# A transformer block with expert routing on one Trainium2 core: the jobs of an expert cut into sixteen equal slots

## The chip, the cores and the metric

The kernel runs on one core of one Trainium2 chip. The metric is the device time of one execution in microseconds (us). The engines are TensorE (PE in the profile, with its weight loads as PEld), VectorE (DVE), ScalarE (ACT), GpSimd (POOL) and SyncE (SP), which here only issues DMAs.

## The reference

The input is 16 sequences of 256 tokens with 256 features (4096 tokens). Attention with 16 heads comes first, then a mixture of 8 experts in which the expert chooses its tokens:

```python
x = x + o @ Wout.T                                    # attention
tok = x.reshape(-1, d)                                # 4096 tokens
gate = softmax(tok @ Wgate.T, axis=-1)                # 4096 x 8
k_cap = bs // E                                       # 512 tokens for an expert
vals, idx = top_k(gate.T, k_cap)
w, idx_flat = vals.T, idx.T.reshape(-1)
g = _ln(tok[idx_flat], mlp_g, mlp_b).reshape(k_cap, E, d)
y = gelu(einsum('ked,ehd->keh', g, fc1s) + b1s)       # 256 -> 1024
y = (einsum('keh,edh->ked', y, fc2s) + b2s) * w[..., None]
tok = tok.at[idx_flat].add(y.reshape(-1, d))
```

All arithmetic that matters for the output is float32. Lists and one-hots of the routing are bfloat16.

## The kernel before, in words

**Two parts of the choice.** The tokens form 32 tiles of 128. The kernel does not wait for the last sequence before it starts the experts: a first routing chooses, for each expert, the best 256 among the first 30 tiles, and a second routing chooses the other 256 among all 32 tiles less those already chosen. That gives 16 jobs of 256 tokens each: jobs 0 to 7 are the eight experts with the first routing (30 tiles), jobs 8 to 15 the eight experts with the second (32 tiles).

**Order of the work.** Each engine works through its instructions in the order in which the Python code emits them. Up to job 0 this order comes from a plan with due times, written out by hand (`at(...)`, sorted in L1064); the change leaves it alone. From L1090 on the order is that of the last loop, `for k in range(1, len(jobs))`. It starts at about 970 us of a span of 1232.7 us.

**A routing.** `Gates` turns the logits of some tiles into gate values: `shift` (VectorE), `exp` (ScalarE), `divide` (VectorE) and `parts` (GpSimd, which splits each gate value into three bfloat16 parts). `Routing.turn` transposes the gate values on TensorE, and `evict` copies them out. Then a binary search over 30 bits finds the threshold of each expert. A bit has four steps: `compare` (VectorE, L776: which values reach the candidate, and how many in each partition), `count` (TensorE, L783: a small bfloat16 product that adds up the partitions), `drop` (VectorE, L788) and `step` (VectorE, L795), which give the next candidate. At the end come `masks` (VectorE), `totals` (TensorE), `place` (VectorE, two scans), `turn_places` (TensorE) and `split` (VectorE), which give each chosen token its place in the list. The second routing runs inside the last loop; `second_routing` is a generator that hands out its steps.

**A job** (class `Job`) consists of these steps:

- `load`: SyncE issues the DMAs of both weights (1 MB each) and of the second bias. Each of the two weight buffers is one of two, so the load of job k+2 waits for the products of job k.
- `gives` (VectorE, L879 and L887): the values that the list product carries, token numbers and gate parts.
- `onehot(a, b)` (VectorE, L897): for the tiles a to b-1 a 128x128 bfloat16 one-hot of each token's place.
- `list_matmul(a, b)` (TensorE, L906): one small bfloat16 product for each tile, a 128x128 one-hot against 10 columns, all added up in one PSUM tile. The result is the list of the job's tokens.
- `take` (VectorE, L914 to L920) copies the list, forms the indices and the weights `w`; `gather` (GpSimd, L925) fetches the 256 normalised tokens by two indirect DMAs.
- `transposes` (TensorE, L934, four) and `evict` (VectorE, L941, two) bring the gathered tokens into the form `xT`.
- `up(f)` (TensorE, L953) for f = 0 to 7: four float32 half products of 256 columns into a PSUM tile; `gelu(f)` (ScalarE, L960).
- `down(i, a, b)` (TensorE, L969) for i = 0 and 1: two half products for each hidden chunk f.
- `finish(i)` (VectorE, L975 and L976): bias and gate weight; `scatter(i)` (GpSimd, L979): an indirect DMA that adds the rows to the output.

**The last loop.** A pass k runs the products of job k (called `a`) and prepares job k+1 (`new`) and job k+2 (`far`). Over the eight up steps it places the second half of the one-hots of `new` (four after each of the first four steps) and its list products (six after each of the first six steps); `take` and `gather` of `new` come after the seventh up step. In the down part it places `transposes` and `evict` of `new` in the middle of the second output half, and the `gives` and first half of the one-hots of `far`, eight in each half. `route_on()` stands ahead of each up step and twice in each down half, 12 times in a pass, and emits one step of the second routing each time: for a bit, `compare` is one step, and `count`, `drop` and `step` together are the next. So a pass does six bits, and the second routing ends in pass 6. In that pass the preparation of job 8, the first with the second routing, stands behind the end of the routing.

Of the kernel before, what the change touches and what calls it, by code (L numbers as in the profile page):

```python
# [25 lines left out]
NT = NTOK // P  # L26
# [3 lines left out]
FC = DD // P  # L30
KC = CAP // P
KL = KC // 2
# [11 lines left out]
def kernel(  # L44
# [329 lines left out]
    if True:  # L374
# [370 lines left out]
        class Routing:  # L745
# [46 lines left out]
            def step(self, n):  # L792

                old, self.cand = self.cand, bit.tile([P, 1], I32, tag="cand", name="cand")
                nc.vector.scalar_tensor_tensor(  # L795
                    self.cand, self.dropped, (1 << n) >> 1, old,
                    ALU.bitwise_or, ALU.bitwise_xor,
                )
# [207 lines left out]
        for b in range(B):  # L1006
# [3 lines left out]
            a = First(b)  # L1010
# [4 lines left out]
            for (g, t), p in its["group"].items():  # L1015
                a = Group(b, g, t)
# [6 lines left out]
            for (d, *ij), p in its["quad"].items():  # L1023
                a = quads[d]
# [6 lines left out]
            for t in range(TB):  # L1031
                a = Tail(b, t)
# [7 lines left out]
        stretches = [Gates(0, n0), Gates(n0, n1), Gates(n1, NT)]  # L1040
# [3 lines left out]
        second = Routing(first)  # L1044
# [5 lines left out]
        jobs = [Job(e, r, n) for r, n in ((first, n1), (second, NT)) for e in range(E)]  # L1050
# [15 lines left out]

        def second_routing():
            a = stretches[2]  # L1070
            yield from (a.shift, a.exp, a.divide, a.parts, second.turn, second.evict)
            for n in range(29, -1, -1):
                yield partial(second.compare, n)

                def decide(n=n):
                    second.count(n)
                    second.drop(n)
                    second.step(n)
                yield decide
            yield from (second.masks, second.totals, second.place, second.turn_places,  # L1080
                        second.split)

        rest = second_routing()

        def route_on(n=1):
            for step in (next(rest, None) for _ in range(n)):
                if step:
                    step()

        jobs[2].load()  # L1090
        jobs[2].gives()
        jobs[2].onehot(0, NT // 2)
        for k in range(1, len(jobs)):
            a = jobs[k]
            new = jobs[k + 1] if k + 1 < len(jobs) else None
            far = jobs[k + 2] if k + 2 < len(jobs) else None
            for f in range(FC):
                route_on()
                a.up(f)
                a.gelu(f)  # L1100
                if new:
                    if f < 4:
                        new.onehot(NT // 2 + 4 * f, NT // 2 + 4 * f + 4)
                    if f < 6:
                        new.list_matmul(6 * f, 6 * f + 6)
                    if f == 6:
                        new.take()
                        new.gather()
            for i in range(KL):
                route_on()  # L1110
                a.down(i, 0, FC // 2)
                if new and i == KL - 1:
                    new.transposes()
                    new.evict()
                route_on()
                if far and k != len(jobs) // 2 - 2:
                    if i == 0:
                        far.gives()
                    far.onehot(i * NT // 4, (i + 1) * NT // 4)
                a.down(i, FC // 2, FC)  # L1120
                a.finish(i)
                a.scatter(i)
            if k == len(jobs) // 2 - 2:
                while (step := next(rest, None)):
                    step()
                far.gives()
                far.onehot(0, NT // 2)
            if far:
                far.load()


# [47 lines left out]
```

## Time and profile before

| what | us |
|---|---|
| median of 3 runs | 1235.27 (1234.18 to 1235.83) |
| profiled execution | 1234.45 |
| its span in the profile | 1232.70 |
| TensorE busy, of the span | 1180.2 (96%) |
| VectorE busy | 773.4 (63%) |
| ScalarE busy | 603.0 (49%) |
| GpSimd busy | 592.6 (48%) |
| first up product of job 1 | 969.98 |
| first up product of job 15 | 1208.97 |
| from the first up product of job 1 to that of job 8 | 123.72 |
| from the first up product of job 8 to that of job 15 | 115.26 |

Durations that the profile gives for one instruction of the expert part: an up half product is busy 393 ns and a weight load 190 ns; both are pipelined, so the step from one start to the next is shorter. A list product is busy 168 ns, a one-hot 259 ns, `compare` 476 ns, `drop` 154 ns, `step` 165 ns.

How to read it: a timeline line has the start in us from the span's start, the length, the engine, the line of the kernel, the operation, the tile written and the tiles read, and a number of instructions (x4). In brackets stands the time for which the engine sat idle just before and what ended that wait. A row by windows has the stretch, its length, and then for each engine the time busy and the number of instructions; after these the granted clock of TensorE (1.00 is full), the busy share of the DMA engines and the rate in GB/s. A line of waits has the waiting instruction, the one it waited for, the total, how often and the longest.

### The profile page before, as it was taken

What the parts mean: (1) busy time and instruction counts of PE and PEld (TensorE: products, weight loads), DVE (VectorE), ACT (ScalarE), POOL (GpSimd) and SP (SyncE); (2) the same over time, 40 slices, a digit from 0 to 9 for tenths busy, and PEclk for the clock granted to TensorE, in tenths of its full rate; (3) what the DMA queues carried; (4) which work ended last, traced back from release to release, by engine and by line L of the source; (5) the groups of instructions that cost most, each with busy time, mean ns of one, the idle gap of its engine ahead of it and who ended that gap; (6) DMA issues with size and microseconds to landing.
All of it is one profiled execution on the core that took longest, in us unless ns stands there. A gap on an engine that the chain in (4) does not pass through costs nothing. (4 is left out here: it accounts for less than half of the span.)

```text
span 1232.7 us, 19466 instructions
## 1 busy us (share of the span) xinstructions
PE 1180.2 (96%) x6784; PEld 814.0 (66%) x6784; DVE 773.4 (63%) x2276; ACT 603.0 (49%) x1669; POOL 592.6 (48%) x818
## 2 busy tenths in 40 slices
PE   6999999999999999999999999999978999999996
PEld 3556666766566666667575766667646777788875
DVE  7556665757566666657665666665776567755551
ACT  2665555555555555555555555657551322122221
POOL 4555555645555555555455555556653232323322
PEclk9999999999999999999999999999997999999999
DMA  5000000000000000000000000000201556556551
GB/s 181 1 1 5 22 10 18 9 18 14 14 27 1 26 5 23 9 18 14 13 15 14 26 6 22 6 14 18 90 1 46 186 140 177 153 161 178 154 164 26
DMA packets 46739, 62.41 MB, mean 51 GB/s; under 512 B 3888, under 2 KB 39984, under 8 KB 46640
## 3 DMA queue, kind: packets, MB, share of 16 engines
q1 hardware_dynamic: 39808, 52.70, 12.8%
q0 software_dynamic: 6144, 8.39, 3.9%
q8 instruction: 54, 0.88, 0.3%
q14 instruction: 45, 0.37, 0.1%
q10 hardware_dynamic: 688, 0.06, 0.0%
HBM read 48.56 MB, written 12.58 MB: 50 GB/s over the span
## 5 line engine op out<-in xcount | busy, mean ns | idle before, releaser
L608 POOL TENSOR_SCALAR pr<-pr,sums 128x256 f32<-128x256 f32 x512 | 240.0, 489 | 275.1 <-DVE sums L604 259.1
L506 PE MATMUL pm<-wq,hT 128*128 128x512 f32 x768 | 356.8, 603 | 5.0 <-DMA wq<-in_wqkvT 3.0
L597 ACT ACTIVATE pr<-sc,nmax 128x256 f32<-128x256 f32 x512 | 236.9, 477 | 161.4 <-DVE nmax L588 147.0
L82 POOL TENSOR_TENSOR ss<-ss,neghalf 128x8 f32<-128x8 f32 x128 | 210.6, 1650 | 97.8 <-DVE ss L527 95.0
L506 PEld LDWEIGHTS pm<-wq,hT 128*128 128x128 f32 x768 | 137.8, 192 | 148.2 <-issue 135.5
L588 DVE TENSOR_REDUCE nmax<-sc 128x2 f32<-128x512 f32 x256 | 164.5, 681 | 44.7 <-PE sc L581 44.5
L960 ACT ACTIVATE hid<-ph,vec 128x256 f32<-128x256 f32 x128 | 60.3, 474 | 212.7 <-PE ph L953 205.3
L523 DVE TENSOR_REDUCE ss<-sq 128x8 f32<-128x512 f32 x128 | 87.4, 682 | 108.8 <-ACT sq L519 108.6
L617 PEld LDWEIGHTS pp<-ident,pr 128*128 128x128 f32 x1024 | 120.0, 144 | 35.0 <-issue 20.1
L617 PE MATMUL pp<-ident,pr 128*128 128x128 f32 x1024 | 140.0, 277 | 3.3 <-ACT pr L597 2.5
L635 PE MATMUL po<-prT,v 128*64 128x256 f32 x1024 | 139.4, 395 | 0.7 <-ACT oT L645 0.7
L953 PE MATMUL ph<-xT,w 128*128 128x256 f32 x512 | 131.7, 393 | 0.1
L581 PE MATMUL sc<-kT,qT 64*128 64x256 f32 x1024 | 130.2, 392 | 0.0
L519 ACT ACTIVATE sq<-pm 128x512 f32<-128x512 f32 x128 | 77.2, 603 | 90.4 <-PE pm L506 89.2
L659 PE MATMUL pw<-wo,oT 128*128 128x256 f32 x512 | 118.5, 384 | 0.0
L581 PEld LDWEIGHTS sc<-kT,qT 64*128 64x128 f32 x1024 | 94.2, 187 | 34.7 <-issue 23.6
L969 PE MATMUL py<-w,hid 128*128 128x256 f32 x512 | 116.9, 381 | 0.0
L979 POOL DMA_INDIRECT out<-y,idx x32 | 51.1, 1598 | 121.4 <-DVE y L976 62.7
L597 ACT ACTIVATION_READ_ACCUMULATOR pr<-sc,nmax 128x1 f32 x512 | 105.9, 207 | 0.0
L659 PEld LDWEIGHTS pw<-wo,oT 128*128 128x128 f32 x512 | 95.7, 192 | 13.0 <-issue 0.8
L625 DVE COPY prT<-pp 128x512 f32<-128x512 f32 x112 | 76.9, 687 | 43.4 <-PE pp L617 42.5
L969 PEld LDWEIGHTS py<-w,hid 128*128 128x128 f32 x512 | 95.6, 190 | 12.7
(118 smaller groups left out, 1312.1 us busy)
## 6 DMA issues: line engine op xcount, KB each, us to landing
w<-in_fc1T SPq DMA_DIRECT2D x16, 1024.0 KB, 5.5
w<-in_fc2T SPq DMA_DIRECT2D x16, 1024.0 KB, 5.6
xs<-in_x SPq DMA_DIRECT2D x16, 256.0 KB, 2.9
out<-tok SPq DMA_DIRECT2D x32, 128.0 KB, 1.7
xn_dram<-tn SPq DMA_DIRECT2D x32, 128.0 KB, 1.7
wq<-in_wqkvT SPq DMA_DIRECT2D x6, 512.0 KB, 8.6
b<-in_b2s SPq DMA_DIRECT2D x16, 128.0 KB, 5.2
wo<-in_woutT SPq DMA_DIRECT2D x1, 1024.0 KB
```

The source lines that it names most:

```text
L82: nc.gpsimd.tensor_tensor(dst, src, neghalf[:, : src.shape[1]], ALU.pow)
L506: nc.tensor.matmul(self.pm, hTs[self.b][:, c, bass.ts(self.t, P)], wq[:, c, bass.ts(self.g, GW)], start=(c == 0), stop=(c == DC - 1),)
L523: nc.vector.tensor_reduce(self.ss[:, 0, :], self.sq.rearrange("p (h d) -> p h d", d=HD), AX.X, ALU.add,)
L581: nc.tensor.matmul(self.sc[i, j][:, t, :], qTs[self.b][rows, hp, bass.ts(t, P)], kTs[self.b][rows, hp, :], start=True, stop=True,)
L588: nc.vector.tensor_reduce(self.nmax[i, j], self.sc[i, j], AX.X, ALU.max, negate=True)
L597: nc.scalar.activation(self.pr[i, j][:, t, :], self.sc[i, j][:, t, :], AF.Exp, bias=self.nmax[i, j][:, t : t + 1], scale=1.0, accum_out=se ...
L608: nc.gpsimd.tensor_scalar(self.pr[i, j][:, t, :], self.pr[i, j][:, t, :], self.sums[i][:, 1, j, t : t + 1], 1.0, ALU.mult, ALU.mult,)
L617: nc.tensor.transpose(self.pp[i, j][:, c, bass.ts(t, P)], self.pr[i, j][:, t, bass.ts(c, P)], ident,)
L635: nc.tensor.matmul(self.po[j * HD : (j + 1) * HD, i, :], vs[self.b][:, c, bass.ts(4 * self.d + 2 * i + j, HD)], self.prT[i, j][:, c, :], s ...
L659: nc.tensor.matmul(self.pw, oTs[self.b][:, hp, bass.ts(self.t, P)], wo[:, hp, :], start=(hp == 0), stop=(hp == HP - 1),)
L953: nc.tensor.matmul(self.ph[f], self.w1[:, c, bass.ts(f, P)], self.xT[:, c, :], start=(c == 0), stop=(c == DC - 1),)
L969: nc.tensor.matmul(self.py[i], self.hid[:, f, bass.ts(i, P)], self.w2[:, f, :], start=(f == 0), stop=(f == FC - 1),)
```

## The change

A pass now has 16 slots: one for each of the eight up steps, and eight for the down part, each with two of the eight hidden chunks of one output half (`down(i, 2 * q, 2 * q + 2)`). `second_routing` yields a list of steps for each slot, and these are emitted at the head of the slot, ahead of its products. A bit takes two slots: in the first stand `count`, `drop` and `step` of one bit and the `compare` of the next, the second is empty. So a pass does eight bits; the whole takes 74 slots, and ends in slot 9 of pass 5. In pass 1 the gate steps stand in slots 0 to 2 and `turn` in slot 4.

The list products of `new` stand in one cluster of 30 or 32 at the head of slot 6, with `take` and `gather` right behind. The one-hots of `new` come four in each of slots 0 to 3, as before. In pass 7, where job 8 is `new` (`late`), `gives` and all 32 one-hots stand in slots 0 to 3, eight in each, and the cluster in slot 7. `transposes` and `evict` of `new` stand at the head of slot 14, in the middle of the second output half as before. For `far`, `gives` stands in slot 9 and the one-hots, four at a time, in slots 10, 12, 13 and 15; pass 6 has none. `finish(0)` and `scatter(0)` stand at the end of slot 11, `finish(1)` and `scatter(1)` at the end of slot 15.

```diff
@@ -1066,27 +1066,21 @@
         def second_routing():
-            a = stretches[2]
-            yield from (a.shift, a.exp, a.divide, a.parts, second.turn, second.evict)
+            a, b = stretches[2], second
+            yield from ([a.shift], [a.exp], [a.divide, a.parts], [], [b.turn], [b.evict])
+            new = [partial(b.compare, 29)]
             for n in range(29, -1, -1):
-                yield partial(second.compare, n)
-
-                def decide(n=n):
-                    second.count(n)
-                    second.drop(n)
-                    second.step(n)
-                yield decide
-            yield from (second.masks, second.totals, second.place, second.turn_places,
-                        second.split)
+                yield new
+                yield []
+                new = [partial(f, n) for f in (b.count, b.drop, b.step)]
+                new.append(partial(b.compare, n - 1) if n else b.masks)
+            yield from (new, [], [b.totals, b.place], [], [], [], [b.turn_places], [b.split])
         rest = second_routing()
-
-        def route_on(n=1):
-            for step in (next(rest, None) for _ in range(n)):
-                if step:
-                    step()
-
+        last = len(jobs) // 2 - 2
         jobs[2].load()
         jobs[2].gives()
         jobs[2].onehot(0, NT // 2)
@@ -1094,39 +1088,41 @@
             a = jobs[k]
             new = jobs[k + 1] if k + 1 < len(jobs) else None
             far = jobs[k + 2] if k + 2 < len(jobs) else None
-            for f in range(FC):
-                route_on()
-                a.up(f)
-                a.gelu(f)
-                if new:
-                    if f < 4:
-                        new.onehot(NT // 2 + 4 * f, NT // 2 + 4 * f + 4)
-                    if f < 6:
-                        new.list_matmul(6 * f, 6 * f + 6)
-                    if f == 6:
-                        new.take()
-                        new.gather()
-            for i in range(KL):
-                route_on()
-                a.down(i, 0, FC // 2)
-                if new and i == KL - 1:
+            late = k == last + 1
+            for s in range(2 * FC):
+                for step in next(rest, ()):
+                    step()
+                if new and s < 4:
+                    if late and s == 0:
+                        new.gives()
+                    h = 0 if late else NT // 2
+                    w = (NT - h) // 4
+                    new.onehot(h + w * s, h + w * s + w)
+                if new and s == (7 if late else 6):
+                    new.list_matmul(0, NT)
+                    new.take()
+                    new.gather()
+                if new and s == 14:
                     new.transposes()
                     new.evict()
-                route_on()
-                if far and k != len(jobs) // 2 - 2:
-                    if i == 0:
+                if far and k != last and s in (9, 10, 12, 13, 15):
+                    if s == 9:
                         far.gives()
-                    far.onehot(i * NT // 4, (i + 1) * NT // 4)
-                a.down(i, FC // 2, FC)
-                a.finish(i)
-                a.scatter(i)
-            if k == len(jobs) // 2 - 2:
-                while (step := next(rest, None)):
-                    step()
-                far.gives()
-                far.onehot(0, NT // 2)
+                    else:
+                        w = {10: 0, 12: 1, 13: 2, 15: 3}[s]
+                        far.onehot(w * NT // 8, (w + 1) * NT // 8)
+                if s < FC:
+                    a.up(s)
+                    a.gelu(s)
+                else:
+                    i, q = divmod(s - FC, 4)
+                    a.down(i, 2 * q, 2 * q + 2)
+                    if q == 3:
+                        a.finish(i)
+                        a.scatter(i)
             if far:
                 far.load()
+        assert next(rest, None) is None
 def kernel(**inputs):
```

## The prediction, made before the change was run

> **What bounds the kernel now.** The change lies in the last fifth of the span, where expert jobs 1 to 15 run one after the other. I write job k for pass k of the last loop, and call its period the time from its first up product to the first up product of job k+1. I read the busy time by windows first, one window per period: span, then TensorE, weight loads, VectorE, ScalarE, GpSimd.
>
> ```profile
> 1023.13:1040.56 17.43, 16.22 (x106) 13.51 (x105) 12.43 (x67) 3.80 (x8) 5.21 (x4) 1.00 0.59 160
> ...
> 1110.36:1126.69 16.33, 15.80 (x102) 13.27 (x101) 8.83 (x45) 3.80 (x8) 5.18 (x4) 1.00 0.59 170
> ...
> 1193.39:1208.97 15.58, 15.58 (x102) 13.32 (x101) 6.24 (x30) 3.80 (x8) 5.18 (x4) 1.00 0.41 105
> ```
>
> These are jobs 4, 9 and 14. TensorE sets the end everywhere; the periods differ by what it waits for. All 14 periods in us: 18.56, 17.36, 17.23, 17.42, 17.14, 17.42, 18.59 (jobs 1 to 7, sum 123.72), 16.65, 16.32, 16.52, 16.39, 17.41, 16.39, 15.58 (jobs 8 to 14). Next TensorE's waits from 970 to 1209 us:
>
> ```profile
> PE px L934 <- DMA xg<-xn_dram,idx: 6.0, 9, 1.6
> PE pc L783 <- DVE reach L776: 4.7, 5, 0.9
> PE pls L906 <- DVE oh L897: 2.5, 4, 1.0
> ```
>
> So: the gather, the search's count, and the one-hots (jobs 1 and 7). Last, the timelines. TensorE in job 9, start and length first:
>
> ```profile
> 1108.25 0.55 PE L934 MATMUL px<-ident,xg 128*128 128x128 f32 x3 [0.86 <-DMA xg<-xn_dram,idx]
> ...
> 1110.36 1.03 PE L953 MATMUL ph<-xT,w 128*128 128x256 f32 x4
> 1111.22 0.30 PE L906 MATMUL pls<-give,oh 128*128 128x10 bf16 x6
> 1111.38 1.11 PE L953 MATMUL ph<-xT,w 128*128 128x256 f32 x4
> ```
>
> An up step is four f32 half products, 0.2155 us apart (0.862). List products follow one another at 0.025. After a cluster the second f32 half comes 0.299 after the first, not 0.2155. So a cluster of n costs 0.087 + 0.025n: six cost 0.24, and 0.862 + 0.24 is the 1.10 from the up step at 1111.38 to the next at 1112.48. The same view of job 4, then VectorE there:
>
> ```profile
> 1025.23 0.16 PE L783 MATMUL pc<-cnt,block 128*128 128x1 bf16 x1 [0.93 <-DVE reach L776]
> ```
>
> ```profile
> 1023.97 0.41 DVE L975 TENSOR_TENSOR y<-py,b 128x256 f32<-128x256 f32 x1
> 1024.42 0.35 DVE L976 TENSOR_SCALAR y<-y,w 128x256 f32<-128x256 f32 x1
> 1024.69 0.47 DVE L776 TENSOR_SCALAR_CACHE_REDUCE reach<-gT,cand 128x256 bf16<-128x256 f32 x1
> ...
> 1025.74 0.15 DVE L788 TENSOR_SCALAR drop<-pc 128x1 int32<-128x1 f32 x1
> ```
>
> The count waits because its compare stands on VectorE behind the last job's `finish`. From start to start: y to scale 0.45, scale to the next 0.27 (finish 0.72); drop to step 0.18, step to compare 0.19, compare to the next 0.40 (a bit 0.77); compare to the count on TensorE 0.54; a one-hot 0.163. The end of a list copies to `ls` 0.21 later, and from `ls` to the second gathered half at TensorE are 7.4 to 8.1 us, 8.7 once. In job 14, with no weights in flight, the gather holds nothing up.
>
> **The Trainium skill.** "TensorE: Matmul & The Clock Gate", section "Wait — 56ns, not 53.3ns?", gives a floor of about 25 ns from product to product, which the trace shows, and about 62 ns a product where the sequencer decodes in software. The trace's longest run at 0.025 is ten; a run of 32 is not shown. Its opening table gives TensorE a queue of 64, and the others one of 8 in strict order; that VectorE works in order is what the lines above show. The same page, "What's actually happening", has the clock halved after an idle window of 3.41 us. The trace has such windows, but half idle is enough (busy TensorE, then its clock):
>
> ```profile
> 896.55:899.96 3.41, 1.39 (x10) 1.00 0.00 0
> 899.96:903.38 3.42, 3.21 (x14) 0.50 0.00 0
> ...
> 1173.03:1176.44 3.41, 1.80 (x11) 1.00 0.38 48
> ```
>
> Busy 1.39 was followed by half clock, and so were 1.66 and 1.49 later (920.44, 940.92); 1.78 (from 893.14) and 1.80 were not.
>
> **The change, part by part.** *Jobs 8 to 14, one cluster.* Six clusters become one: 5 x 0.087 = 0.435 saved. The one-hots are in place: finish ends 0.9 into the job (on VectorE only four far one-hots stand ahead of it now), the 16 left take 2.6, so 3.6, and the cluster comes after six up steps, at 5.17. Is the gain eaten by the gather? List end, gather, and the weight load behind the eighth up step all move by the same 0.435, and TensorE's work from list end to transposes is unchanged, so the wait of 0.1 to 1.9 there stays as it is. VectorE's new order (eight one-hots between finish and evict) is done 7.5 after list end, the transposes at 8.5. On GpSimd the gather stays behind the same scatter; SP's loads keep their place. 7 x 0.435 = **3.05 saved**.
>
> *Job 6.* The search ends in slot 9 of job 5 (74 slots, 16 a job), so job 6 has neither search nor far one-hots: list end 5.17 + 0.78 = 5.95, second gathered half 5.95 + 0.21 + 7.7 = 13.86, next job 0.28 + 1.83 later: 15.97. **1.45 saved**.
>
> *Job 7.* gives and all 32 one-hots lie in its slots 0 to 3: finish 0.92, gives 0.80, one-hots 5.12 (jitter of the same 32 in job 7 of before), 0.30 to TensorE: list end 7.14, 0.3 later than slot 7 alone gives. + 0.21 + 7.6 + 0.28 + 1.83 = 17.06; the gather now starts with the weight load and not ahead of it, 0 to 0.6 more; I take 0.14: 17.2. **1.39 saved**.
>
> *Jobs 2 to 4, eight bits each, not six.* A wait in order again, now: drop blocks VectorE's queue, and behind it stand compare, the one-hots and evict. I walk VectorE from the count of slot 12 (time 0). finish(0) is ready at 0.20, drop 0.92, compare done 1.69, eight one-hots 2.99, drop and compare of slot 14 3.77, evict (TensorE had its transposes at 2.85, gather included) to 4.68, next job's up at 4.81, four one-hots 5.33, finish 6.05, compare at TensorE: count of slot 2 at 6.96. Then eight one-hots and a bit, 2.07, against two slots and a count on TensorE, 1.84: count of slot 4 at 9.03, of slot 6 at 11.10, list end 11.85, slot 8 at 13.68, and slot 12, 3.67 later, at 17.35. That is the period, against 17.34 on average now: eight counts and VectorE's chain eat the 0.35 of the clusters. **0.04 lost** over three jobs.
>
> *Job 5.* The masks take 0.8 in place of a compare, so totals start about 0.6 after TensorE is there; `place` (2.84, as in job 6 of before) now stands ahead of `take` on VectorE, which starts 1.2 after list end + 0.21. The gather is late by that: 18.28. **1.14 lost**.
>
> *Job 1.* Up to gate_of VectorE's queue is the same, so turn cannot start before it does now:
>
> ```profile
> 976.47 0.51 PE L757 MATMUL pgT<-ident,gate_of 128*128 128x128 f32 x2 [0.19 <-DVE gate_of L727]
> ```
>
> What filled TensorE till then, 24 list products and the waits for them, is gone: it is through up steps 0 to 3 at about 973.6 and idles 2.9. The lists come after turn: list end 979.25, not 977.81; with VectorE's chain as above, 8.48 from the count of slot 8 to the next up: 19.58. **1.02 lost**. And 2.9 idle: unless the free-running window splits it evenly, one window has under 1.7 busy, and half clock follows: 3.41 x 0.5 = 1.7 at most, nothing if split. Bounds 0 and 1.7; about four in five positions trigger it; I take **1.4 lost**, an estimate.
>
> Sum: 3.05 + 1.45 + 1.39 - 0.04 - 1.14 - 1.02 - 1.4 = **2.3 us saved**. The profiled execution took 1234.45 (span 1232.70 and 1.75 around it), so 1232.15 there; the median of the runs is 0.8 above it: 1235.27 - 2.3 = **1233.0 us**.
>
> **The unknown costs.** Products 11 to 32 of a cluster: 25 ns (none in the trace is faster) to 62; I take 25, since a queue of 64 holds 32 pairs and TensorE runs 0.2155 a pair before them. VectorE's walk: half a microsecond a job either way.
>
> **Rivals.** *B, slower: the cluster starves.* If TensorE's queue holds few pairs, products past the tenth come at 62 ns: 37 x 22 x 14 = 11.4, thus 1244. It decides from 7.5 ns more per product (308 of them) on, and is slower by 0.2% from 15.5. For it: no run over ten. Against: runs of ten at 0.025 without a sign of tiring. *C: two slots are enough.* If VectorE's chain does not bind, jobs 2 to 4 fall to the gather's floor (list end 6.17, + 0.21 + 7.55 + 0.28 + 1.83 = 16.04), 3.9 less: 1229.1. Against it stand finish and eight one-hots in the queue. *D: the change doesn't do what it says,* jobs 8 to 13 keep their periods since the gather lands when the weights are through: 6 x 0.435 given back, 1235.6. Job 14, without weights, speaks for it; that the load moves along speaks against. *E:* more half-clock windows or a later gather in jobs 5 and 7: 1236 to 1238.
>
> **Chances.** Forecast 0.62 (own range 1231 to 1235), B 0.12, C 0.13, D 0.06, E 0.07. About 0.2%, 2.5 us, is what a measurement can tell from no change: under 1232.8 is faster. The forecast straddles it: 0.30 faster, 0.31 same, 0.01 slower; C faster; B 0.10 slower, 0.02 same; D same; E 0.05 slower, 0.02 same: 0.43, 0.41, 0.16. Range 1229 to 1237: it leaves out most of B, half of C and some of E, 0.19.
>
> **What would show it.** Right: list runs of 32 at 0.025 and periods 0.435 shorter in jobs 8 to 14; turn still near 976.5 with 2.9 idle before it, half clock behind; jobs 2 to 4 near 17.35 with counts waiting 0.2 to 0.4 for reach; `ls` waiting behind `place` in job 5. Wrong: spacing over 0.03 inside the cluster, search jobs near 16, or clean jobs with a longer gather wait than now.

## The result, and the profile after

The changed kernel takes 1229.72 us (median of 5 runs, 1227.31 to 1231.03) beside 1235.83 of the kernel before (5 runs): ratio 0.9951, 95% interval 0.9936 to 0.9965, so 6.1 us faster, with 4.3 and 7.9 as the ends. The forecast was 1233.0 and 2.3 us faster. The direction and the range held; the size was off by nearly 4 us, and 1233.0 itself lies outside the interval.

The profiled execution took 1229.52 us, its span 1227.8. Busy times are nearly those of before (TensorE 1175.4, VectorE 777.0). The windows of jobs 4, 9 and 14 after the change, columns as before:

```profile
1023.93:1041.13 17.20, 16.36 (x108) 13.27 (x107) 14.23 (x75) 3.79 (x8) 5.20 (x4) 1.00 0.55 162
...
1108.29:1124.21 15.92, 15.35 (x101) 13.30 (x100) 9.02 (x45) 3.79 (x8) 5.17 (x4) 1.00 0.61 174
1188.77:1203.91 15.14, 15.14 (x102) 13.35 (x100) 5.68 (x26) 3.79 (x8) 5.18 (x4) 1.00 0.42 108
```

Job 14 is 0.44 shorter, as forecast, and job 4 hardly changed although it now does eight bits. TensorE's waits in the whole stretch (968 to 1204 us) show what changed places:

```profile
PE px L934 <- DMA xg<-xn_dram,idx: 6.9, 8, 1.7
PE pgT L757 <- DVE gate_of L727: 2.9, 1, 2.9
PE pc L783 <- DVE reach L776: 2.4, 4, 0.6
PE po L813 <- DVE mask L806: 0.5, 1, 0.5
PE ph L953 <- DVE xT L941: 0.5, 3, 0.2
```

The wait of the lists for one-hots is gone, that of the count is halved, and a new one of 2.9 us stands ahead of turn in job 1. TensorE's timeline in job 9:

```profile
1106.18 0.55 PE L934 MATMUL px<-ident,xg 128*128 128x128 f32 x3 [0.78 <-DMA xg<-xn_dram,idx]
...
1108.29 5.34 PE L953 MATMUL ph<-xT,w 128*128 128x256 f32 x24
1113.47 0.95 PE L906 MATMUL pls<-give,oh 128*128 128x10 bf16 x32
1114.27 1.97 PE L953 MATMUL ph<-xT,w 128*128 128x256 f32 x8
```

All 32 list products run in 0.80 us up to the next up product, 0.025 each to the last: no product of the cluster is slower. The wait for the gather stays.

To see what repeats, both kernels were profiled a second time in the experiments. The periods in us, as in the prediction:

| jobs | before | before again | forecast | after | after again |
|---|---|---|---|---|---|
| 1 | 18.56 | 18.55 | 20.98 | 20.91 | 19.22 |
| 2 to 4 | 52.01 | 52.64 | 52.05 | 51.63 | 51.63 |
| 5 | 17.14 | 17.23 | 18.28 | 17.35 | 17.55 |
| 6 | 17.42 | 17.42 | 15.97 | 16.03 | 15.85 |
| 7 | 18.59 | 20.03 | 17.2 | 17.64 | 17.56 |
| 8 to 14 | 115.26 | 115.10 | 112.21 | 111.76 | 111.61 |
| 1 to 14 | 238.98 | 240.97 | 236.69 | 235.32 | 233.42 |

The means of the last row differ by 5.6 us, which is most of the measured 6.1. The rest can't be read from four traces: the stretch ahead of job 1, which the change leaves alone, scatters by 4 us (job 1 begins at 969.98 and 966.17 us in the traces of before, at 968.59 and 970.23 in those of after).

### The profile page after: what moved, and what is told of

Its sections match the earlier page's. It is cut to its first block, busy times and chain, and to the rows that moved or that the text cites. A ratio compares the mean times of both kernels' runs of the same rounds, so it can differ in the third digit from the quotient of the medians.

```text
span 1227.8 us, 19464 instructions
## 1 busy us (share of the span) xinstructions
PE 1175.4 (96%) x6784; PEld 812.7 (66%) x6784; DVE 777.0 (63%) x2276; ACT 602.2 (49%) x1669; POOL 590.7 (48%) x818
## 5 line engine op out<-in xcount | busy, mean ns | idle before, releaser
L953 PE MATMUL ph<-xT,w 128*128 128x256 f32 x512 | 121.0, 388 | 0.6 <-DVE xT L941 0.5
L953 PEld LDWEIGHTS ph<-xT,w 128*128 128x128 f32 x512 | 95.7, 192 | 17.8 <-issue 3.5
```

The source lines that it names most:

```text
L953: nc.tensor.matmul(self.ph[f], self.w1[:, c, bass.ts(f, P)], self.xT[:, c, :], start=(c == 0), stop=(c == DC - 1),)
```

## The experiments

All edits but one are made to the changed kernel. The ratio is to the kernel before, timed on the same chip; its medians were 1234.6, 1234.7, 1235.7 and 1234.6 in the four groups of runs. The groups ran on three chips, so kernels of two groups are best compared by their ratios. The trace of a kernel is one execution.

### Both kernels again

No edit.

> The changed kernel once more, nothing edited, to see what repeats. Theory (the change saves about 3.7 us in jobs 1 to 14, the rest of the measured 6.1 is spread of the runs and of waits on gathers): 3 to 7 us under the kernel before; in the trace job 1 takes 20.5 to 21 with 2.9 us idle ahead of turn, jobs 2 to 5 take 17.2 to 17.4, and the periods of jobs 7 to 13 scatter by some tenths with the gather. First up product of job 1 anywhere between 968 and 970.5, since nothing ahead of it was changed. Rival (the change does something ahead of job 1): it stands near 968.6 again, and that of the kernel before near 970 in every trace.

> The kernel before once more, nothing edited. Theory (what lies ahead of job 1, and the gather's landing, scatter from run to run): within 1.5 us of the other runs of the kernel before; the first up product of job 1 between 968 and 971, job 12 near 16.5 and not 17.4 again, the other periods within 0.5 us of the first trace. Rival (these differences belong to the kernel): job 1 begins near 970.0 and job 12 takes 17.4 again.

The changed kernel: 1227.82 us, ratio 0.9943 (0.9923 to 0.9963). The kernel before: 0.9996 (0.9985 to 1.0008). The first up product of job 1 stood between 966.2 and 970.3 in all traces of this study: the spread ahead of job 1 is not the change's, though it is wider than expected (the second trace of before begins at 966.17, below the 968 given). Two periods missed as well: job 1 of the changed kernel took 19.22, not 20.5 to 21, and job 7 of the kernel before 20.03, not within 0.5 of 18.59; both are a matter of half clock, below. And job 12 was wrong: it took 17.41, 17.54, and 17.25 in the cluster-alone kernel below, that is, in every kernel with the old places of the one-hots, and 15.4 to 16.6 in all others. There the second gathered half of job 13 lands 8.7 to 9.0 us after its `ls` (the copy of the list), elsewhere 7.4 to 8.3. The line from the trace of before:

```profile
1174.89 0.55 PE L934 MATMUL px<-ident,xg 128*128 128x128 f32 x3 [1.61 <-DMA xg<-xn_dram,idx]
```

So about 1.1 us of the gain is this one gather. It goes with the slots and not with the cluster, as the traces of both parts alone show (one each, below); why it does is open.

### The cluster in jobs 8 to 14

```diff
                 if new and s == (7 if late else 6):
-                    new.list_matmul(0, NT)
+                    if not (k > 7):
+                        new.list_matmul(0, NT)
...
                     a.up(s)
                     a.gelu(s)
+                    if new and (k > 7) and s < 6:
+                        new.list_matmul(6 * s, 6 * s + 6)
```

> The changed kernel, but in passes 8 to 14 the list products stand six behind each of the first six up steps, as before the change. Theory (each cluster costs TensorE 0.087 us beside 0.025 per product, and the gather moves along with the list's end): those seven periods are 0.435 longer each, 3.0 us in all. Rival (the gather lands when the weights are through, and takes the clusters' gain back): jobs 8 to 13 keep their periods, only job 14 is 0.44 longer, and the time moves by less than 0.6 us.

1232.61 us, 0.9980 (0.9971 to 0.9989), 4.8 slower than the changed kernel beside it. Jobs 9 to 14 take 98.05 us, 6 x 0.40 more than the 95.62 of the first trace after (6 x 0.46 more than the second), and job 14 alone 0.44 more. A half-clock window behind the wait of job 7 adds 0.8 to job 7 and as much to job 8, and is more than half of the 1.4 by which job 8 is longer; how often it falls in the other runs, and so how much of the 4.8 it makes, is not known. The theory holds; the rival, no change in jobs 8 to 13, falls.

### The wait ahead of turn, two ways

Lists of pass 1 spread (the edit of the last experiment with `k == 1` for `k > 7`), and TensorE kept at work:

> The changed kernel, but in pass 1 alone the 30 list products stand six behind each of the first six up steps, as before the change. Theory (clustering left TensorE nothing to do ahead of turn, which VectorE sets): job 1 falls from 20.9 to about 18.2 us (the idle stretch of 2.9 is gone, no window of half clock behind it, the list ends 1.5 us sooner), so 2.7 us faster. Rival (turn sets the job's length, whatever lies ahead of it): within 0.5 us of the changed kernel.

```diff
+            def fill():
+                idle = ps.tile([P, CAPL], F32, tag="mm", bufs=3, name="idle")
+                for _ in range(6):
+                    nc.tensor.matmul(
+                        idle, jobs[1].w1[:, 0, :P], jobs[1].xT[:, 0, :], start=True, stop=True
+                    )
-            yield from (..., [b.turn], [b.evict])
+            yield from (..., [fill, b.turn], [b.evict])
```

> The changed kernel with six float32 products of 128x256 on TensorE, into a tile that nobody reads, ahead of turn in pass 1: 2.6 us of the 2.9 that TensorE idles there are filled, and turn starts when it did. Theory (a window that is half idle is followed by half clock, which costs up to 1.7 us here): no half clock after it, job 1 about 19.5 in place of 20.9, 1.4 us faster. Rival (half clock costs nothing, the job waits for VectorE and the gather anyway): job 1 stays at 20.9 though the clock is full.

Half clock is a granted clock of 0.50. In the traces it begins at the edge of a regular stretch of 3.41 us, and such a stretch is called a window here.

Spread: 1225.86 us, 0.9930 (0.9911 to 0.9950); job 1 takes 18.78, with no half clock. Filled: 1225.66, 0.9928 (0.9910 to 0.9945); job 1 takes 19.28, with no half clock. Both medians are about 2 us under the changed kernel beside them, though the intervals overlap. TensorE in the spread kernel, then in the filled one:

```profile
973.35 0.51 PE L757 MATMUL pgT<-ident,gate_of 128*128 128x128 f32 x2 [0.19 <-DVE gate_of L727]
```

```profile
970.07 2.75 PE L1076 MATMUL idle<-xT,w 128*128 128x256 f32 x12
973.20 0.48 PE L757 MATMUL pgT<-ident,gate_of 128*128 128x128 f32 x2 [0.38 <-DVE oh L897]
```

Turn comes 6.5 to 6.6 us into the job in both: VectorE sets it. The half clock is best read from the two traces of the changed kernel. Windows of the clock, TensorE's busy time and then the clock, first trace and second:

```profile
975.08 0.55 PE L757 MATMUL pgT<-ident,gate_of 128*128 128x128 f32 x2 [2.88 <-DVE gate_of L727]
```

```profile
972.00:975.42 3.42, 0.54 (x3) 1.00 0.82 236
975.42:978.83 3.41, 3.41 (x10) 0.50 0.32 34
```

```profile
971.87:975.28 3.41, 1.98 (x10) 1.00 1.00 323
975.28:978.70 3.42, 1.98 (x10) 1.00 0.29 52
```

The same wait of 2.88 falls into one window in the first and into two equal parts in the second. The first is followed by half clock, the second is not: job 1 takes 20.91 and 19.22, so half clock costs 1.69 here. Of the seven traces of kernels with this wait and no filler, six have half clock behind it; job 1 took 20.29 to 20.74 in the other five. Beside the 19.22 without half clock the filled kernel wins nothing in job 1 and the spread kernel 0.4, so what both gain there is mainly that half clock stayed away: the filler's theory holds and its rival falls, while the spread's 2.7 was too much. (The filled kernel's job 2 takes 18.28, 1.1 longer, with a late gather.) And spreading doesn't rule half clock out: in the kernel with all lists spread, below, job 1 takes 19.85 with a half-clock window in it.

### Job 8 prepared like the others

```diff
-        last = len(jobs) // 2 - 2
+        last = -2
```

> The changed kernel without the special case of job 8: its gives and the first half of its one-hots stand in slots 9 to 15 of pass 6 like those of every other job, and its list cluster in slot 6 of pass 7. Theory (job 7 is long since 32 one-hots stand ahead of the cluster and the gather starts a slot late): job 7 falls from 17.6 to 16.1 us, job 6 stays at 16.0, so 1.5 us faster. Rival (job 7 waits for its gather behind the weights either way): job 7 stays above 17 us.

1227.12 us, 0.9942 (0.9924 to 0.9961): not to be told from the changed kernel. Job 7 takes 16.84 in place of 17.64. The list ends sooner, but TensorE now waits 1.64 for the gather, which lands 8.57 after `ls`. Half of the 1.5 us came, half went to the gather: 16.84 lies between the 16.1 of the theory and the 17 of the rival, and neither holds as stated.

### The cluster one slot earlier

```diff
-                if new and s == (7 if late else 6):
+                if new and s == (7 if late else 5 if k > 7 else 6):
```

> The changed kernel, but in passes 8 to 14 the cluster with take and gather stands in slot 5, one slot earlier. Theory (in jobs 8 to 13 TensorE waits 0.7 to 1.1 us at the transposes, and the gather's landing counts from the list's end): the gather lands 0.86 sooner against TensorE's work, those waits fall to 0 to 0.3, jobs 8 to 13 take 15.2 to 15.4, 4 to 5 us faster in all; job 14 is unchanged. Rival (the gather lands when the weight loads are through, whenever it starts): the waits stay at 0.7 to 1.1 and the time within 0.6 us.

1226.86 us, 0.9938 (0.9919 to 0.9958), so 1 us, which the timing can't resolve. In the trace jobs 8 to 13 take 93.09, not 96.62, and the waits of TensorE at the transposes of jobs 9 to 14, in the changed kernel and then here:

```profile
PE px L934 <- DMA xg<-xn_dram,idx: 4.5, 6, 0.9
```

```profile
PE px L934 <- DMA xg<-xn_dram,idx: 0.9, 3, 0.5
```

From the starts of the transposes the mean wait falls from 0.91 to 0.32, by 0.59 of the 0.86 moved; the gather lands 8.10 after `ls` in place of 7.83. So two thirds of the move reached TensorE, and the jobs take 15.3 to 15.8, not 15.2 to 15.4. The rival is not refuted in full: what holds back the rest may be the load beside the gather (last section).

### VectorE's chain in the search jobs

```diff
-                        w = {10: 0, 12: 1, 13: 2, 15: 3}[s]
+                    if k < 6:
+                        w = {9: 0, 10: 1, 12: 2, 15: 3}.get(s)
```

> The changed kernel, but in passes 1 to 5 the four far one-hots of slot 13 stand in slot 9 behind gives. Theory (in jobs 2 to 5 a chain on VectorE, finish, one-hots, two bits, evict, finish, a bit, sets the count of slot 2, not TensorE): evict and all behind it come 0.65 sooner, the wait ahead of the count of slot 2 shrinks from about 0.75 to 0.1, jobs 2 to 5 take 16.6 to 16.8 in place of 17.2 to 17.4, 2 to 2.6 us faster. Rival (the gather or TensorE's own work holds these jobs): within 0.5 us of the changed kernel.

1224.43 us, 0.9918 (0.9900 to 0.9936), 3.4 under the changed kernel's 1227.82, though the intervals of the two ratios overlap. In the trace jobs 2 to 5 take 67.03, not 68.98, which is 1.95 of it and about the 2 to 2.6 of the theory; but jobs 3 and 5 (17.02 and 17.26) fell less than expected, jobs 2 and 4 (16.57 and 16.18) as much or more. TensorE's waits in jobs 2 to 5, in the changed kernel and then here:

```profile
PE pc L783 <- DVE reach L776: 2.4, 4, 0.6
PE po L813 <- DVE mask L806: 0.5, 1, 0.5
PE ph L953 <- DVE xT L941: 0.5, 3, 0.2
```

```profile
PE pc L783 <- DVE reach L776: 0.8, 3, 0.3
PE po L813 <- DVE mask L806: 0.5, 1, 0.5
```

Four one-hots moved, and the waits for reach and xT shrink by 2.1: the chain of the prediction held these jobs, and the rival falls.

### The slots without the cluster, and the cluster without the slots

The first has the edit of the first spread kernel with `not late` for `k > 7`. The second is made to the kernel before:

```diff
             for f in range(FC):
                 route_on()
+                if new and f == 6:
+                    new.list_matmul(0, NT)
+                    new.take()
+                    new.gather()
                 a.up(f)
                 a.gelu(f)
...
-                    if f < 6:
-                        new.list_matmul(6 * f, 6 * f + 6)
-                    if f == 6:
-                        new.take()
-                        new.gather()
```

> The changed kernel with the slots and the search as they are, but the list products spread over the first six slots in every pass but pass 7: the slots alone, without the cluster. Theory (the parts add up): against the changed kernel 3.0 us lost in jobs 8 to 14, 0.35 in job 6, 0 to 0.35 in each of jobs 2 to 5, and 2.7 won in job 1: about 1 us slower than the changed kernel, and still 3 to 5 us faster than the kernel before, from the shorter search, job 6 and job 7. Rival (the cluster is what makes the kernel faster): back at the time of the kernel before.

> The kernel before with its two steps of the search a bit and its places of one-hots, but with the list products in one cluster ahead of the seventh up step: the cluster without the slots. Theory: 3.0 us won in jobs 8 to 14 and about 1.4 in job 7, 0.7 to 2.3 lost in job 1, where TensorE idles ahead of turn and half clock may follow, and nothing in jobs 2 to 6, where the cluster's gain turns into a longer wait for the count: 2 to 4 us faster than the kernel before. Rival (search jobs also gain 0.35 each): 4 to 6 us faster.

Slots alone: 1227.81 us, 0.9932 (0.9917 to 0.9948), as fast as with the cluster. Cluster alone: 1233.46 us, 0.9987 (0.9977 to 0.9997). Both expectations missed, and so did both rivals. With the slots alone, the trace shows against the first trace of before 2.8 us won in jobs 6 and 7, 1.8 in jobs 2 to 5 and 1.3 in jobs 8 to 14 (most of it job 12), and 1.3 lost in job 1 with its half clock. Jobs 2 to 5 were not a little longer than in the changed kernel but shorter: 67.31, not 68.98. TensorE there, job 4's first count:

```profile
1024.35 0.16 PE L783 MATMUL pc<-cnt,block 128*128 128x1 bf16 x1 [0.22 <-DVE reach L776]
```

In the changed kernel the same count waits longer:

```profile
1026.52 0.16 PE L783 MATMUL pc<-cnt,block 128*128 128x1 bf16 x1 [0.59 <-DVE reach L776]
```

The list products of the first slots lie inside that wait. In a cluster they come after it, and the 0.75 us of 30 products is paid in full, for 0.35 of clusters saved. In the cluster-alone kernel jobs 8 to 14 take 112.47, 2.8 less than before, and job 7 takes 16.96, 1.6 less; job 1 with half clock takes 2.0 more; and jobs 2 to 6 take 88.79, not 86.57: the list ends later, and TensorE waits up to 1.0 for the gather and 5.3 in all for the count (4.7 before). So against the first trace of before the cluster gains 4.4 us where the search has ended (jobs 7 to 14), and gives 4.2 back where it has not.

### Edits put together

A first attempt, with five edits, and a second:

```diff
-        last = len(jobs) // 2 - 2
+        last = -2
...
-                if new and s == (7 if late else 6):
-                    new.list_matmul(0, NT)
+                if new and s == (5 if k > 5 else 6):
+                    if not (k < 6):
+                        new.list_matmul(0, NT)
...
-                        w = {10: 0, 12: 1, 13: 2, 15: 3}[s]
+                    if k < 6:
+                        w = {9: 0, 10: 1, 12: 2, 15: 3}.get(s)
...
                     a.gelu(s)
+                    if new and (k < 6) and s < 6:
+                        new.list_matmul(6 * s, 6 * s + 6)
```

(That is the second; the first spread the list products in pass 1 alone, and the one-hots of passes 2 to 5 at three a slot over six slots.)

> The changed kernel with five edits together: the lists of pass 1 spread; job 8 prepared in passes 6 and 7 like every other; the cluster in slot 5 from pass 6 on; no far one-hots in slot 13 of passes 1 to 5; and in passes 2 to 5 the second half of the one-hots at three a slot over six slots. Theory (each of these waits was ended last by what the edit moves): 2.7 + 1.5 + 5.5 + 2.4 + 1.0, about 13 us faster than the changed kernel. Rival (a wait taken away uncovers the next one, above all the gather): half of that or less.

> The five edits again with two of them changed: the list products are spread over the first six slots in all of passes 1 to 5, where TensorE waits for VectorE anyway, and the second half of the one-hots stays at four a slot. Theory (with the one-hots at three a slot those of slots 4 and 5 stood behind place in pass 5, and the cluster waited 1.3 us for them; spread list products fill waits in search jobs that a cluster leaves empty): job 5 falls from 18.7 to 16.3 to 16.9, jobs 2 to 4 take 16.0 to 16.5, about 2 us faster than the first attempt at putting the edits together. Rival (the length of job 5 is its late gather): job 5 stays above 18.

First: 1221.69 us, 0.9887 (0.9870 to 0.9904), 6 us in place of 13, since waits added up less than their sum: job 5 took 18.74, its cluster 1.2 behind one-hots that stood behind `place`, and job 7 still waited 1.8 for its gather. The rival of the first holds: it got half. The theory of the second holds: job 5 took 16.33. Second: 1219.16 us, 0.9873 (0.9850 to 0.9895), the fastest kernel here, 15.5 us under the kernel before. Jobs 2 to 5 take 16.3 to 16.5. Its waits from 966 to 1194 us:

```profile
PE px L934 <- DMA xg<-xn_dram,idx: 3.2, 7, 0.7
PE pls L906 <- DVE oh L897: 1.2, 2, 0.9
PE px L934 <- issue: 0.5, 1, 0.5
PE pgT L757 <- DVE gate_of L727: 0.2, 1, 0.2
```

No wait for reach is left among them; the gather is what remains.

## Why the prediction was right in direction and short in size

By the means of the table the forecast is short by 3.3 us: 0.9 in job 1, 0.7 in jobs 2 to 4, 0.9 in job 5, 0.3 in job 7 and 0.4 in jobs 8 to 14.

**Jobs 8 to 14 (forecast 3.05, measured 3.5).** The step held: 0.435 a job, undone by spreading at 0.40 to 0.46. Two terms were not in the sum. Job 12's long gather (1.1) went, and what is left over says that the gathers of the other jobs held TensorE 0.13 longer each (0.7 in all), a small piece of rival D. These two have opposite signs, so that the total comes near 3.05 is in part luck. Rival D saw the gather rightly, for it lands with the load of weights (last section); but the load moved along, as the forecast argued against it: it starts 7.99 us into jobs 8 to 13 and not 8.42. Rival B is refuted: 32 products at 0.025.

**Job 6 (1.45; measured 1.5) and job 1 (lost 1.02 and 1.4 for half clock; measured 0.66, and 1.69 where the clock falls).** The mechanism was right, with the start of turn, the idle 2.9 and the evenly split window as forecast. Whether half clock falls is chance from one execution to the next, and it fell in one of the two traces.

**Jobs 2 to 4 (0.04 lost; 0.7 won) and job 5 (1.14 lost; 0.3 lost).** The walk along VectorE was right link by link up to one. It has the counts of slots 2, 4 and 6 at 6.96, 9.03 and 11.10 us behind the count of slot 12 of the job before; in job 4 they come 6.99, 9.08 and 10.93 behind it. The mis-sized term is the number of one-hots: these lists have 30 tiles, so slot 3 has two one-hots and not four. VectorE in job 4:

```profile
1028.47 1.06 DVE L897 TENSOR_SCALAR oh<-lane,partf 128x128 bf16<-128x128 bf16 x6
1029.45 0.15 DVE L788 TENSOR_SCALAR drop<-pc 128x1 int32<-128x1 f32 x1
```

Six, where the walk had eight: 0.33 less, so the count of slot 6 does not wait, and the period is 17.2, not 17.35. That is 0.4 of the 0.7; for the rest, the second trace of before has longer jobs 2 to 4 than the first. In job 5 the list ended later than forecast, but `take` stood behind `place` by 0.77 and not 1.2:

```profile
1049.47 0.42 DVE L829 TENSOR_TENSOR place<-place 128x256 f32<-128x256 f32 x1
1049.81 0.16 DVE L914 COPY ls<-pls 128x10 f32<-128x10 f32 x1
```

So `ls` comes 8.68 into the job, about where the forecast had it (8.62, which is 18.28 less 1.83, 0.28 and 7.55). The term that was mis-sized in job 5 is the gather: it landed 6.6 and 6.8 after `ls` in the two traces, not 7.55.

**Job 7 (1.39; measured 1.0).** The list ended as walked (7.20 against 7.14), but the gather lands 8.1 to 8.2 after `ls`, not 7.7: the upper end of the bound given. The base is uncertain as well: in the second trace of before, job 7 pays 1.4 for a half-clock window of its own. The sum charged half clock to the changed kernel alone, on one trace of before. Between the first pair of traces (3.7) and the means (5.6) half clock is the largest item: 0.85 since the second trace of after has none in job 1, 0.7 since the second trace of before has one in job 7. How often each occurs is not shown by two traces.

**What the forecast did not see.** It booked the cluster as the largest gain (3.05 in jobs 8 to 14, though the 2.4 lost in job 1 are the cluster's too) and 1.7 for all of jobs 2 to 7. The runs of the parts say otherwise: the slots without the cluster give all of the measured gain, 4.7 us of it in jobs 2 to 7 of their trace against the first of before, and the cluster adds nothing to it; alone it gives 1.6 us by its ratio (0.4 to 2.8). The slots hold several changes at once (the shorter search, the places of the one-hots, job 8's preparation), and no run separates these.

## What to carry to other kernels

Small products on TensorE are worth a cluster only where TensorE would otherwise not wait; where it waits for another engine anyway, spread small products fill that wait free of charge, so ask of each stage what its wait ends on before regrouping. Walk the in-order queue of the engine that ends the wait with its exact counts (the last slot of a shorter list here), since two instructions fewer decided whether a count waited. Measure a gather that runs beside a bulk load against the end of that load, and not only against its own start. And a moved wait of some 3 us is not only its own length: see what share of one clock window it fills, in the kernel before as well.

## What the runs showed of the hardware that was not expected

- Half clock follows a window in which TensorE's work is small and not only one that looks empty. The Trainium skill, TensorE: Matmul & The Clock Gate, section "What's actually happening", puts half clock after an idle window. Here a window with 0.54 of 3.42 us busy was followed by half clock and one with 1.98 was not, so it need not be wholly idle; the measurement decides. No threshold comes out: over all traces, windows at full clock without list products in them went both ways from 1.63 to 1.85 us busy. In the second trace of before the window ahead of job 7's half clock shows 2.10 us busy, more than the two windows of 1.98 above, which had none:

```profile
1072.14:1075.55 3.41, 2.10 (x13) 1.00 0.74 204
1075.55:1078.97 3.42, 3.42 (x20) 0.50 0.73 205
```

  Six of its products are list products, which the records count busy for 0.17 us each though they can follow one another at 0.025. That they count for little towards the clock would explain it. The traces agree with it elsewhere: in twelve of the fourteen, a window near 938 us with 26 or 27 list products shows 2.2 to 2.6 us busy and half clock follows, while of the windows without list products none above 1.85 was followed by half clock. In the trace of after:

```profile
937.87:941.28 3.41, 2.47 (x31) 1.00 0.00 0
941.28:944.69 3.41, 1.93 (x7) 0.50 0.00 0
```

  No run changed the list products of such a window to try it.
- The second gathered half mostly lands with the load of the next weights, and not a fixed time after `ls`. In the first trace of after it lands 0.26 to 0.43 us after the load of the first weights (`fc1T`) in jobs 1 to 4, 6 and 8 to 13, and 0.66 after it in job 5. From `ls` TensorE sees it 7.6 to 8.0 us later in jobs 8 to 13, but 6.6 in job 5, where `ls` stands 2.5 us later in the job and the load's end only about 1. In job 14, without such a load, the half lands 2.8 us after its issue, where jobs 8 to 13 have 5.1 to 5.5. There are exceptions: job 7 lands 1.94 after the load, job 2 of the filled kernel 1.84 and job 7 of the first attempt at the edits together 1.61, and job 1 of the kernel with all lists spread, whose second half is issued 0.7 ahead of the load, lands 2.2 before the load's end. Why these differ is open, and no run moved the load alone, so which of the two holds up the other is not shown.
